# Loading the weights of a GRU kernel one contraction part at a time

## The chip, the core and the metric

The kernel runs on one core of a Trainium2 chip. The metric is device time in microseconds (us) of one execution. The core has TensorE (PE) for products, VectorE (DVE), ScalarE (ACT), GpSimd (POOL) and SyncE (SP). SP, ACT and POOL also issue DMA transfers, which sixteen DMA engines carry out.

## The reference

`x` has 16 sequences of 256 steps with 512 channels. It first goes through a causal depthwise convolution with 16 taps, taken from `cond`, and is added to itself. Then a GRU runs over the 256 steps, starting from `cond`, and its states are added again.

```python
x = x + conv(x, cond[:, None, :])            # 16 taps, per channel, causal
# per step, h from the step before, D = 512:
gi = x_t @ W_ih + b_ih                       # W_ih, W_hh: 512 x 1536, gates r, z, n
gh = h @ W_hh + b_hh
r = sigmoid(i_r + h_r); z = sigmoid(i_z + h_z)
n = tanh(i_n + r * h_n)
h = (1 - z) * n + z * h
x = x + h over all steps
```

All of it is float32. The weights are 6 MB, `x` is 8 MB.

## The kernel before

Channels are on partitions. A channel's number is j * 128 + q * 32 + l; it sits on partition 32 j + l in part q. So a product over all 512 channels is four products, kc = 0 to 3, one for each part q, and a weight tile such as `whh[g]` is [128 partitions, 4 parts, 512 columns], with row j * 128 + q * 32 + l of the matrix on partition 32 j + l, part q. There are five weight tiles: `wih_n` and `wih_rz` (the latter 1024 columns wide, two gates) for the input, and `whh[R]`, `whh[N]`, `whh[Z]` for the state.

`x` comes in 16 chunks of 16 steps. `load_x(c)` brings one chunk in eight transfers of 64 KB. `turn_units` transposes a chunk on VectorE, and `tap_units` adds the convolution's taps there (L265), one instruction for each tap and part. Chunk 0 has half of its convolution on TensorE (`conv_on_tensor`, L292). Three buffers hold loaded chunks.

The order on each engine is written out by hand (`manual_schedule`). The kernel has a head and then 256 steps. In the head, `mark` and `idle_products(PAD)` give TensorE small products at the very start (L356). Then come the convolution of chunk 0, the biases, the input products of n for the first eight steps (`ni_units`, L320, with `wih_n`) and those of r and z for the first pair of steps (`pair_units`, L383, with `wih_rz`). `bulk.run(0, HEAD)` then puts taps of chunk 1, up to a planned cost of `HEAD` us, on VectorE ahead of step 0; `Plan` hands the rest to the steps by their deadlines.

A `step` makes the state's products in the order r, n, z (`recurrent`, L418, 16 products for each gate, kc outside and j inside), then a share of the input products of later steps. ScalarE makes r (L435), VectorE r times the n products (`rn`, L444), its transpose, the sum `n`, ScalarE the tanh (L455) and z (L461), and VectorE the new state by a scan (L470). The next step's products wait for that.

The DMA issues stand in the queues in program order. SP has part of `cond`, of chunk 0 and chunk 1, the biases, the first two quarters of `wih_n` and of `wih_rz`, then one quarter of each `whh`, then chunk 4 (issued when chunk 1 is transposed), then chunks 2 and 3 (which wait for z of step 1), and later all other chunks and the stores. POOL has part of chunks 0 and 1, the other two quarters of every weight tile, and two memsets of `zero_z` between them. ACT has one quarter of each `whh`. The framework numbers the transfers over eight lanes for SP and ACT together and eight for POOL; a transfer waits for the one before it in its lane to land.

A quarter here is a j: 32 partitions, on each of them four pieces (q) of 512 or 1024 columns.

Of the kernel before, what the change touches and what calls it, by code (L numbers as in the profile page):

```python
# [30 lines left out]
P = 128  # L31
L = 32
GT = 8
R, Z, N = 0, 1, 2
CHUNKS = (16,) * 16
PAD = 108
HEAD = 9.3
SYNC = mybir.DependencyInfo(mybir.DependencyClass.Sync, mybir.DependencyReason.DATA)
Q_PE = (2, 3)
NI = 8  # L40
# [35 lines left out]
def conv_gru_kernel(  # L76
# [10 lines left out]
    nc = tc.nc  # L87
    B, T, C = x.shape
    K = cond.shape[0]
    NQ = C // P  # L90
# [4 lines left out]
    GP = GT // 2  # L95
    NG = T // GT
    NCH = len(CHUNKS)
# [21 lines left out]
    def load_x(c, queues=((nc.sync,), (nc.sync,)), behind=None):  # L119

        n = CHUNKS[c]
        t = xin.tile([P, max(CHUNKS) // 2, P], F32, tag="x_nat", name=f"x_nat_{c}")
        for s in range(2):
            for j in range(NQ):
                made = queues[s][j % len(queues[s])].dma_start(
                    out=t[32 * j + B * s : 32 * j + B * s + B, 0 : n // 2],
                    in_=x[:, starts[c] + s : starts[c] + n : 2, j * P : (j + 1) * P],
                )
                if s == j == 0 and behind is not None:
                    tc.add_manual_dep(made.ins, behind.ins.name, SYNC, reason="later in time")  # L130
        x_nat[c] = t
# [8 lines left out]
    for j in range(NQ):  # L140
        (nc.sync, nc.scalar)[j % 2].dma_start(
            out=cond_nat[32 * j : 32 * j + B, :], in_=cond[:, j * P : (j + 1) * P]
# [17 lines left out]
        out=b_two[1:2, 0 : 2 * C], in_=b_ih[0 : 2 * C].rearrange("(o c) -> o c", o=1)  # L160
    )
    nc.gpsimd.dma_start(
        out=bn_nat[0:P:L, :], in_=b_ih[2 * C : 3 * C].rearrange("(j c) -> j c", j=NQ)
# [3 lines left out]
    wih_rz = const.tile([P, NQ, 2 * C], F32)  # L167
    wih_n = const.tile([P, NQ, C], F32)
    whh = [const.tile([P, NQ, C], F32, name=f"whh_{g}") for g in range(3)]

    def load_weights(w_sb, w, g, queues):
        for j in (0, 2, 1, 3):
            queues[j].dma_start(
                out=w_sb[L * j : L * j + L],
                in_=w[j * P : (j + 1) * P, g * C : g * C + w_sb.shape[2]].rearrange(
                    "(q l) c -> l q c", l=L
                ),
            )


    for tile_of, g in ((wih_n, N), (wih_rz, R)):
        load_weights(tile_of, w_ih, g, (nc.sync, nc.sync, nc.gpsimd, nc.gpsimd))
    zero_z = [const.tile([P, NQ * B * 2], F32, name=f"zero_z_{i}") for i in range(2)]
    for t in zero_z:
        nc.gpsimd.memset(t, 0.0)
# [26 lines left out]
    def turn_units(c):  # L212

        def halo():
            xT[c] = xtp.tile([P, NQ, HALO + CMAX], F32, tag="xT", name=f"xT_{c}")
            if c:
                m = CHUNKS[c - 1] * B
                nc.scalar.copy(xT[c][:, :, 0:HALO], xT[c - 1][:, :, m : m + HALO])

        def turn(a):  # L220
            o = HALO + a * PAIR
            nc.vector.transpose(
                xT[c][:, :, o : o + GT * B].rearrange("p q (a r) -> p a q r", r=L),
                x_nat[c][:, a : a + GP].rearrange("p a (q l) -> p a q l", q=NQ),
            )
            if 2 * (a + GP) == CHUNKS[c] and 3 < c + 3 < NCH:
                load_x(c + 3)

        return [(0.0, halo)] + [
            (0.7, lambda a=a: turn(a)) for a in range(0, CHUNKS[c] // 2, GP)  # L230
        ]
# [46 lines left out]
    def conv_on_tensor():  # L278

        n = CHUNKS[0] * B  # L280
        diag = const.tile([P, len(Q_PE), K, P], F32)

        def weight(k, q):
            return condT[:, q, k : k + 1] if k < K - 1 else last1[:, q : q + 1]

        for i, q in enumerate(Q_PE):
            for k in reversed(range(K)):
                nc.scalar.activation(diag[:, i, k], ident, AF.Copy, scale=weight(k, q))
        for i, q in enumerate(Q_PE):
            acc = ps_ni.tile([P, CHUNKS[0] * B], F32, tag="pni", name=f"conv_{q}")  # L290
            for k in reversed(range(K)):
                nc.tensor.matmul(  # L292
                    acc[:, lag(k) : n],
                    lhsT=diag[:, i, k],
                    rhs=xT[0][:, q, HALO : k * B + n],
                    start=(k == K - 1),
                    stop=(k == 0),
                    skip_group_check=True,
                )
            evictions.append(lambda q=q, acc=acc: nc.scalar.copy(x1T[0][:, q, 0:n], acc[:, 0:n]))  # L300
# [46 lines left out]
    def mark():  # L347

        for i in range(2):
            nc.tensor.matmul(rz[i], lhsT=blank[:, 0:P], rhs=blank, start=True, stop=True)  # L350
            nc.tensor.matmul(nh[i], lhsT=blank[:, 0:P], rhs=blank[:, 0:P], start=True, stop=True)

    def idle_products(n):

        for _ in range(n):
            nc.tensor.matmul(  # L356
                spare[0:L, 0, 0:1], lhsT=blank[:, 0:L], rhs=blank[:, 0:1], start=True, stop=True
            )
# [17 lines left out]
    def pair_units(p):  # L376

        c, o = chunk_of(2 * p)

        def prod(kc):  # L380
            w_rz = wih_rz[:, kc].rearrange("p (g c) -> p g c", g=2)
            for j in range(NQ):
                nc.tensor.matmul(  # L383
                    rz[p % 2][32 * j : 32 * j + 32],
                    lhsT=x1T[c][:, kc, o : o + PAIR],
                    rhs=w_rz[:, :, j * P : (j + 1) * P],
                    start=False,
                    stop=False,
                    skip_group_check=True,
                )  # L390

        return [lambda kc=kc: prod(kc) for kc in range(NQ)]
# [143 lines left out]
    mark()  # L536
    idle_products(PAD)
    nc.tensor.drain()
# [14 lines left out]
                last1[:, q : q + 1],  # L553
            )
    conv_on_tensor()
    for g in (R, N, Z):

        load_weights(whh[g], w_hh, g, (nc.sync, nc.scalar, nc.gpsimd, nc.gpsimd))

    taps = [fn for i, (_, fn) in reversed(list(enumerate(tap_units(0)))) if i % NQ not in Q_PE]  # L560
    needed = (NI - 1) * (NQ - len(Q_PE))
# [23 lines left out]
    for c in range(1, NCH):  # L585
# [9 lines left out]
        if c == 1:  # L595
            for cost, fn in ahead:
                bulk.add(cost, due + GT // 2, fn)
    bulk.run(0, HEAD)

# [3 lines left out]
    for t in range(T):  # L603
        p, s = divmod(t, 2)
        if s == 0 and p + 1 < T // 2:
            of_pair = pair_units(p + 1)
        if t % NI == 0 and t + NI < T:
            of_block = ni_units(*blocks[t // NI + 1])

        def other_products():  # L610

            for units in (of_pair, of_block):
                for _ in range(2):
                    if units:
                        units.pop(0)()

        def bulk_work():

            quota = bulk.rate(t) + 2 * 0.7 / GT
            room = ROOM  # L620
            while late and (t >= T - 2 or room == ROOM):
                cost, fn = late.pop(0)
                fn()
                quota -= cost
                room -= cost
            bulk.run(t, quota, room)

        h = step(t, h, bulk_work, other_products)
        if t == 1:

            load_x(2, behind=of_z[0])
            load_x(3)
        if t == T - 3:
            late += out_units(NG - 1, 0, GP - 1)
        elif t % GT == GT - 1 and t < T - 1:
            late += out_units(t // GT)
        elif t == T - 2:
            late += out_units(NG - 1, GP - 1, GP, (0,))
# [30 lines left out]
```

## Time and profile before

| | |
|---|---|
| Median of three runs | 1045.49 us (1044.62 to 1045.6) |
| The profiled execution | 1043.0 us, its span 1041.2 us |
| Granted TensorE clock, mean | 0.999 |
| Busy | PE 98%, DVE 89%, ACT 37%, POOL 1% |
| HBM | 14.73 MB read, 8.39 MB written |

Times are from the start of the span. "Busy" is the time in which an engine has an instruction in execution. In the group rows the last column is the time for which the engine stood idle ahead of them, and what ended it. A DMA's time to landing runs from its issue to its completion. Here are the weights' issues:

| tile | issued by | number, size | median us to landing |
|---|---|---|---|
| wih_n | SP / POOL | 2 / 2, 256 KB | 8.8 / 7.7 |
| wih_rz | SP / POOL | 2 / 2, 512 KB | 15.3 / 11.3 |
| whh | SP / ACT / POOL | 3 / 3 / 6, 256 KB | 18.1 / 12.7 / 16.9 |

### The profile page before, as it was taken

Reading aid. Unit: us, or ns where it says so; the run is one execution under the profiler, and the core shown is the slowest. Engines: PE = TensorE matmul, PEld = TensorE weight load, DVE = VectorE, ACT = ScalarE, POOL = GpSimd, SP = SyncE. Lnnn points to the kernel's source line nnn. Section 1 sums busy time; section 2 is a strip of 40 time slices with the busy share of each in tenths; the row PEclk is TensorE's granted clock in tenths of the full one; section 3 lists DMA queues with packets and bytes.
Section 4 is the critical chain, followed back from the end, with each engine's and each line's share of the span. In section 5 each row is a group of like instructions: output and inputs, shape, how many; then the busy total and the mean of one; then the engine's idle time right before and its main releaser. Section 6 shows DMA issues by size and latency. Waiting matters only on the chain.

```text
span 1041.2 us, 71851 instructions
## 1 busy us (share of the span) xinstructions
PE 1021.8 (98%) x32952; PEld 927.2 (89%) x32952; DVE 925.6 (89%) x3606; ACT 380.5 (37%) x1520; POOL 11.4 (1%) x27
## 2 busy tenths in 40 slices
PE   7899999999999999999999999999999999999997
PEld 6689999999999999999999999999999999999986
DVE  7799999999999999999999999999999999896555
ACT  6243433434333343433334333343333334333332
POOL 4000000000000000000000000000000000000000
PEclk9999999999999999999999999999999999999999
DMA  9510100100010010100100010010000000000000
GB/s 222 124 38 8 31 14 20 30 15 26 13 34 15 15 34 6 35 14 15 35 14 25 14 33 17 14 35 5 14 15 14 14 13 6 14 15 14 14 10 17
DMA packets 40978, 27.72 MB, mean 27 GB/s; under 512 B 6686, under 2 KB 38498, under 8 KB 40676
## 3 DMA queue, kind: packets, MB, share of 16 engines
q1 hardware_dynamic: 38612, 18.52, 8.0%
q8 instruction: 257, 4.21, 1.8%
q0 software_dynamic: 1216, 3.67, 1.4%
q10 hardware_dynamic: 848, 0.95, 0.4%
q14 instruction: 45, 0.37, 0.1%
HBM read 14.73 MB, written 8.39 MB: 22 GB/s over the span
## 4 chain that ended last, share of the span: by engine, by line
PE 94%; DMA 3%; DVE 1%; ACT 0%; issue 0%; ACTq 0%; SPq 0%
PE prz L418 42%; PE pnh L418 21%; PE prz L383 20%; PE pni L320 10%; DMA whh<-in_L_cond_W_hh_dram 2%; DMA wih_n<-in_L_cond_W_ih_dram 1%; DMA x_nat<-in_x_dram 0%; DVE rn L444 0%; DVE rnT L446 0%; DVE zp L457 0%; ACT zero_z L461 0%; DVE n L448 0%; DMA out_dram<-o 0%; DVE hist L470 0%; DVE glance L398 0%
## 5 line engine op out<-in xcount | busy, mean ns | idle before, releaser
L418 PE MATMUL prz<-whh,hist 128*32 128x128 f32 x16320 | 539.4, 273 | 2.2 <-DVE hist L470 1.0
L418 PEld LDWEIGHTS prz<-whh,hist 128*32 128x32 f32 x16320 | 449.7, 104 | 7.5 <-DVE hist L470 5.2
L265 DVE SCALAR_TENSOR_TENSOR x1T<-xT,condT,x1T 128x256 f32<-128x256 f32 (+2 forms) x930 | 377.4, 461 | 0.6 <-ACT x1T L239 0.6
L383 PE MATMUL prz<-wih_rz,x1T 128*32 128x256 f32 x4096 | 267.8, 379 | 2.6 <-DMA wih_rz<-in_L_cond_W_ih_dram 2.6
L418 PE MATMUL pnh<-whh,hist 128*32 128x128 f32 x8160 | 269.5, 273 | 0.0
L418 PEld LDWEIGHTS pnh<-whh,hist 128*32 128x32 f32 x8160 | 226.5, 104 | 0.0
L455 ACT ACTIVATE dn<-n 128x64 f32<-128x64 f32 x256 | 67.9, 265 | 327.2 <-DVE n L448 327.2
L383 PEld LDWEIGHTS prz<-wih_rz,x1T 128*32 128x32 f32 x4096 | 128.3, 110 | 46.6 <-issue 2.9
L320 PEld LDWEIGHTS pni<-x1T,wih_n 128*32 128x32 f32 x4096 | 122.3, 110 | 43.0 <-ACT x1T L300 0.6
L435 ACT ACTIVATE r<-prz 128x128 f32<-128x128 f32 x256 | 71.1, 278 | 238.4 <-PE prz L418 235.6
L320 PE MATMUL pni<-x1T,wih_n 128*32 128x128 f32 x4096 | 157.6, 273 | 0.0
L470 DVE TENSOR_TENSOR_SCAN hist<-zero_z,dn 128x32 f32<-128x32 f32 (+1 forms) x768 | 128.6, 216 | 0.0
L444 DVE TENSOR_TENSOR rn<-r,pnh 128x128 f32<-128x128 f32 x256 | 72.2, 282 | 39.1 <-PE pnh L418 37.9
L461 ACT ACTIVATE zero_z<-zp 128x32 f32<-128x32 f32 x512 | 90.9, 226 | 8.7 <-DVE zp L457 2.1
L446 DVE STREAM_TRANSPOSE rnT<-rn 128x128 f32<-128x128 f32 x256 | 79.8, 312 | 8.8
L457 DVE STREAM_TRANSPOSE zp<-prz 128x128 f32<-128x128 f32 x256 | 80.8, 316 | 2.0 <-PE prz L418 2.0
L332 ACT ACTIVATE ni<-pni,bnT 128x128 f32<-128x128 f32 x128 | 47.2, 368 | 74.7 <-PE pni L320 74.7
L463 DVE TENSOR_TENSOR dn<-hist,dn 128x64 f32<-128x64 f32 x255 | 58.3, 229 | 11.7
L448 DVE TENSOR_TENSOR n<-rnT,ni 128x64 f32<-128x64 f32 x256 | 57.6, 225 | 8.9
L398 DVE COPY glance<-r 1x1 f32<-1x1 f32 x256 | 34.0, 133 | 26.4 <-ACT r L435 26.4
L371 ACT COPY prz<-b_rows 128x256 f32<-128x256 f32 x128 | 48.5, 379 | 0.0
L398 DVE COPY glance<-zero_z 1x1 f32<-1x1 f32 x256 | 36.3, 142 | 7.9 <-ACT zero_z L461 0.2
(51 smaller groups left out, 208.7 us busy)
## 6 DMA issues: line engine op xcount, KB each, us to landing
out_dram<-o SPq DMA_DIRECT2D x248, 32.0 KB, 1.7
x_nat<-in_x_dram SPq DMA_DIRECT2D x118, 64.0 KB, 2.9
whh<-in_L_cond_W_hh_dram POOLq DMA_DIRECT2D x6, 256.0 KB, 16.9
wih_rz<-in_L_cond_W_ih_dram POOLq DMA_DIRECT2D x2, 512.0 KB, 11.3
wih_rz<-in_L_cond_W_ih_dram SPq DMA_DIRECT2D x2, 512.0 KB, 15.3
whh<-in_L_cond_W_hh_dram ACTq DMA_DIRECT2D x3, 256.0 KB, 12.7
whh<-in_L_cond_W_hh_dram SPq DMA_DIRECT2D x3, 256.0 KB, 18.1
x_nat<-in_x_dram POOLq DMA_DIRECT2D x8, 64.0 KB, 5.4
```

What stands on the lines that cost most here:

```text
L265: nc.vector.scalar_tensor_tensor(out=x1T[c][:, q, to], in0=xT[c][:, q, k * B + to.start : k * B + n], scalar=condT[:, q, k : k + 1], in1=x ...
L320: nc.tensor.matmul(hold[q][32 * j : 32 * j + 32, 0:n], lhsT=wih_n[:, kc, j * P + q * L : j * P + q * L + L], rhs=x1T[c][:, kc, o : o + n], ...
L383: nc.tensor.matmul(rz[p % 2][32 * j : 32 * j + 32], lhsT=x1T[c][:, kc, o : o + PAIR], rhs=w_rz[:, :, j * P : (j + 1) * P], start=False, st ...
L398: nc.vector.tensor_copy(glances[i][0:1], of_scalar[0:1, 0:1])
L418: product = nc.tensor.matmul(dst[32 * j : 32 * j + m], lhsT=h[0](kc), rhs=whh[g][:, kc, j * P : (j + 1) * P], start=False, stop=(kc == NQ ...
L435: of_r = nc.scalar.activation(r, pr, AF.Sigmoid)
L444: nc.vector.tensor_mul(rn, r, pnh)
L446: nc.vector.transpose(rnT, by_part(rn))
L455: nc.scalar.activation(dn_v[:, :, :, 1], n, AF.Tanh)
L457: nc.vector.transpose(zp, by_part(pz))
L461: nc.scalar.activation(z_v[:, qs, :, 1], zp[:, qs, half], AF.Sigmoid) for qs in halves
L470: nc.vector.tensor_tensor_scan(hist_g[:, lo + at : lo + end], z[:, to], dn[:, to], 0.0, op0=ALU.mult, op1=ALU.add,)
```

## The change

Each weight transfer now brings one part q of the rows to all 128 partitions, instead of one j (32 partitions) with all four parts. Parts 0 and 2 go on SP, 1 and 3 on POOL; ACT issues none. All five tiles are issued in one go, in the order in which they are used, ahead of the memsets of `zero_z` and of the convolution. The places of the data in SBUF, and the sizes of the transfers, stay. Chunk 4 is no longer requested when chunk 1 is transposed but behind chunks 2 and 3, at z of step 1. `HEAD` goes from 9.3 to 11.0, and `PAD`, the number of idle products, from 108 to 112.

```diff
-PAD = 108
-HEAD = 9.3
+PAD = 112
+HEAD = 11.0
...
-    def load_weights(w_sb, w, g, queues):
-        for j in (0, 2, 1, 3):
-            queues[j].dma_start(
-                out=w_sb[L * j : L * j + L],
-                in_=w[j * P : (j + 1) * P, g * C : g * C + w_sb.shape[2]].rearrange(
-                    "(q l) c -> l q c", l=L
-                ),
-            )
-
-
-    for tile_of, g in ((wih_n, N), (wih_rz, R)):
-        load_weights(tile_of, w_ih, g, (nc.sync, nc.sync, nc.gpsimd, nc.gpsimd))
+    def load_weights(w_sb, w, g):
+
+        for q in range(NQ):
+            (nc.sync, nc.gpsimd)[q % 2].dma_start(
+                out=w_sb[:, q],
+                in_=w[:, g * C : g * C + w_sb.shape[2]].rearrange(
+                    "(j q l) c -> q j l c", q=NQ, l=L
+                )[q],
+            )
+
+    load_weights(wih_n, w_ih, N)
+    load_weights(wih_rz, w_ih, R)
+    for g in (R, N, Z):
+        load_weights(whh[g], w_hh, g)
...
-            if 2 * (a + GP) == CHUNKS[c] and 3 < c + 3 < NCH:
+            if 2 * (a + GP) == CHUNKS[c] and 4 < c + 3 < NCH:
                 load_x(c + 3)
...
     conv_on_tensor()
-    for g in (R, N, Z):
-
-        load_weights(whh[g], w_hh, g, (nc.sync, nc.scalar, nc.gpsimd, nc.gpsimd))
...
             load_x(2, behind=of_z[0])
             load_x(3)
+            load_x(4)
```

## The prediction, made before the changed kernel ran

> **What bounds the kernel now.** I read the page's groups first, then the chain of waits of the first 42 us, then the DMA view of the same stretch, and last the queue rows.
>
> ```profile
> PE 1021.8 (98%) x32952; PEld 927.2 (89%) x32952; DVE 925.6 (89%) x3606; ACT 380.5 (37%) x1520; POOL 11.4 (1%) x27
> ...
> L418 PE MATMUL prz<-whh,hist 128*32 128x128 f32 x16320 | 539.4, 273 | 2.2 <-DVE hist L470 1.0
> ...
> L383 PE MATMUL prz<-wih_rz,x1T 128*32 128x256 f32 x4096 | 267.8, 379 | 2.6 <-DMA wih_rz<-in_L_cond_W_ih_dram 2.6
> ```
>
> TensorE is busy nearly all the time, and the idle column says that over 256 steps it hardly waits (2.2 us before L418, half of it near the end). From the first product on the new state (37.66 us) to the end there are 255 steps in 1003.5 us, 3.94 us each, all products. Nothing in the diff touches those. So the change is worth what it does to the moment at which the last weights of step 0 are there. The chain of waits shows that moment:
>
> ```profile
> 7.17 11.41 DMA wih_n<-in_L_cond_W_ih_dram
> 18.57 0.02 issue
> 18.59 16.77 DMA whh<-in_L_cond_W_hh_dram
> 35.36 0.14 issue
> 35.49 1.07 PE prz L418 x32
> ```
>
> The z products of step 0 (35.49) wait for the last quarter of the z weights, which SP issued at 18.59, late, because it had to wait for wih_n to land (the waits of SP's queue: L173 waited for wih_n twice, 5.3 us the longer time). What the transfers wait for is the DMA engines themselves. From 10 to 34 us:
>
> ```profile
> DMA  9999999999999999999999999999999999999999
> GB/s 198 229 188 201 201 236 273 290 273 300 239 266 317 294 297 352 317 307 259 345 273 280 239 314 307 283 307 314 318 318 304 300 297 307 289 262 157 118 163 172
> ...
> q0 software_dynamic: 921, 3.10, 48.2%
> q1 hardware_dynamic: 1669, 2.49, 44.6%
> q10 hardware_dynamic: 432, 0.79, 11.9%
> ```
>
> All sixteen engines are full from 10 to 34 us. The head is bound by transfers, and a full engine moves 300/16 = 19 GB/s in the better slices. So the question is: on how many engines does a transfer of the new shape run?
>
> **How many engines a transfer takes.** The page's queue row for SP counts packets, and I can take them apart.
>
> ```profile
> q1 hardware_dynamic: 38612, 18.52, 8.0%
> ```
>
> SP issues 118 loads of x at 128 pieces of 512 B (15104), its stores (31 groups x 8 x 64 pieces, then 384, 64 and 32: 16352), seven weight transfers of 128 pieces (896), two of cond (32) and two of b_two (2). That is 32386. The remaining 6226 are completions: 389 transfers with 16 or 32 outer rows at 16 each are 6224, and 2 are left, one for each one-row b_two. So a transfer posts one completion for each engine it runs on; 16 or 32 outer rows take sixteen engines, one row takes one.
>
> The old weight transfer has outer count 32 on both sides (l, then q). The new one has 128 partitions on the SBUF side, and on the DRAM side j, l, c, whose outer count is 4 and can't be merged with the 32 (768 KB against 6 KB steps). No row shows two sides that differ. The bounds are four engines, if the smaller side decides, and sixteen, if the SBUF side does. I take four: b_two is the only row with an outer count under 16, and it ran on as many engines as that count. Nor does a row show whether four would be the same ones from one SP transfer to the next. If they changed in turn, the load would be even again, which is rival one's arithmetic; if not, it piles up. I take the same four, as a fixed place for each outer index is the plainer arrangement, and leave the other to the chances.
>
> The Trainium skill ("DMA: Bandwidth & Descriptors", section on why a DMA increments its semaphore by 16) speaks against this change: the engine count is the largest number up to 16 that divides the slowest dimension of both patterns, and on the hardware queues they are the lowest-numbered ones. By it every new SP transfer would sit on the same four engines; its ceiling of about 27 GiB/s an engine would make the 46 us below some 34, an estimate from that page that nothing here shows.
>
> **The change part by part.**
>
> *Weights in four engines.* SP carries half of the weights: two parts of each of wih_n, wih_rz and three whh, 0.52 + 1.05 + 3 x 0.52 = 3.15 MB. POOL carries as much. If its transfers also take four engines but in turn, or sixteen, a quarter of that, 0.79 MB, falls on SP's four. So 3.93 MB must pass four engines before the last z part of SP. Rate: in the stretch 24.5 to 29.9 us sixteen engines moved 306 GB/s, so four move 76.5 under load; at best a 2 KB packet of the trace took 84 ns, which is 24.4 GB/s an engine or 98 for four. With twelve engines nearly idle I take a value between, 85. That gives 3.93 MB / 85 GB/s = 46.2 us (bounds 40.3 and 51.4). The first wih_n packets on SP flow at about 8.0 us (issued 6.79 to 8.50), so the last z part lands at 54.2 instead of 35.36: +18.9 us.
>
> *Parts by kc.* `recurrent` goes through kc = 0 to 3 and each new transfer is one kc. When the last part lands (kc 2; kc 3 is POOL's), half of the 32 z products are done: 1.07 / 2, -0.5 us. In the before state the last quarter of j held up all 32.
>
> *Clock.* Between the parts TensorE would sit idle for 3 to 4 us at a time. The trace has one such case: the conv products began after 4.37 us idle, and their first half (32 records) took 6.0 us, the second half with the same shapes 4.65.
>
> ```profile
> L292 PE MATMUL conv<-xT,diag x64: 262/281/763, 9.4 to 19.8; 128*128 128x256 f32 x4, 128*128 128x240 f32 x4, 128*128 128x224 f32 x4, 128*128 128x208 f32 x4
> ```
>
> The 763 ns (a 128x256 product, 379 at L383) is the slow start. The granted-clock column says 1.00 throughout, so only the durations show it. One such start after the last wait: +1.4 us (0 to 1.7). The waits before it cost nothing more, as the last landing covers them.
>
> *HEAD 11.0.* `bulk.run(0, HEAD)` puts 32 taps of chunk 1 ahead of step 0 instead of 28, four more at 0.41 to 0.46: 1.7 to 1.85 us on VectorE. They ended at 30.34, and now at about 32.2. The first rn waits for the n weights, at 33.73 before and by the sum not before 45: cost nothing. With all weights there by 32 us they would be the next bound (rival one). The taps taken out of the later steps free VectorE, which TensorE doesn't wait for.
>
> *Fifth x chunk.* Eight loads, 0.52 MB, leave SP's place behind the weights (22.84 to 35.68) and come after chunks 2 and 3 at step 1. On sixteen full engines six of them took 0.39 MB / 300 GB/s = 1.3 us of the weights' time. With four engines the gain is a few tenths of that (they follow the weights on the queue), so nothing. Chunks 2 and 3 took SP 10.4 us (41.2 to 51.6); with chunk 4 about 16, from about 61 to 77. Chunk 2's transposes come in step 5 or later, now a step earlier for the four taps, more than 8 us after its own loads; chunk 4 is needed tens of steps later. Stores, which queue behind on SP, start at step 8 (about 88 us). Nothing waits.
>
> *Queues and the rest.* ACT loses three issues (0.3 to 0.45 us each, its sequencer ran ahead), SP's z issues wait for wih_n to land, about 15 us, and their packets would queue behind wih_rz anyway. POOL's two memsets of zero_z go behind its last issue, at 16 us or somewhat later; first use is at 37. Four more idle products are 4 x 28 ns in a gap of 4.37 us. All nothing.
>
> Sum: 18.9 - 0.5 + 1.4 = +19.8 us. On the profiled execution (1043.0 us; span 1041.2) that is 1062.8. The runs' median is 1045.49, 2.5 above the profiled one, so 1065.3.
>
> **The rivals.**
>
> One, all sixteen engines take part (other side: faster). For it: the SBUF side has 128 partitions, and each DMA has the same 256 or 512 KB. Then 0.39 MB of x no longer stand in the way (-1.3 us), and if 128 partitions take 300 GB/s where 8 to 14 us showed 206, another 0.56 MB / 300 = -1.9. The last z part then lands at 32.2 to 34; VectorE, free at 32.2 instead of waiting for 33.73, allows -1.5, and the rest only as far as z is the later. I put -2.2: 1043.3 (1041.5 to 1045). It decides if the last whh lands before 35.36. Against it: b_two's completion counts. 0.15.
>
> Two, four engines only for SP, and the packets at their shortest (84 ns for 2 KB), with POOL's share out of the way by other engines: 3.15 MB / 98 = 32.1, landing at 40.1, +4.7 - 0.5 + 0.7 = +5, 1050. This is the low end of the slower case. Part of the 0.81 below.
>
> Three, POOL's transfers too stay on those four: 6.3 MB / 85 = 74 us, +47 us, 1092. Nothing in the trace speaks for it, software transfers share evenly now. 0.04 within the slower case.
>
> Four, the two effects cancel, because eight engines share the load or the clock is kept: 1044 to 1047. 0.04.
>
> **How the numbers follow.** Four engines, in its variants: 0.81; no change: 0.04; sixteen: 0.15. 0.2% of 1045, about 2 us, is what a measurement of this kernel can tell from no change. The likeliest case with its bounds of rate (40.3 to 51.4 us) and clock gives +12.5 to +25.3, 1058 to 1071; POOL's unknown share stretches it to 1050 below and, with some of POOL's engines shared twice, 1084 above. The faster case is left out of the range, with the extreme of rival three: 0.2.
>
> **What would show it.** Right: the SP queue's row reads 38612 + 3 x 128 pieces - 112 + 40 completions = 38924 (39044 with sixteen engines); the DMA row falls to 3 to 5 tenths after some 25 us; SP's last whh takes over 30 us from issue to landing; the chain ends its DMA stretch at 48 to 60 us; the first products after it are slow for some 3 us; from there steps of 3.94 us. Wrong: DMA at 9 tenths to the end of the head, and z of step 0 before 36 us; or SP's transfers on four engines but over 100 GB/s for them.

## The result, and the profile after

The changed kernel's median is 1076.87 us, the kernel before in the same series 1045.18 us: ratio 1.0296, 95% interval 1.0279 to 1.0313. The median is of four executions, 1073.49, 1076.59, 1077.14 and one of 1221.54 at a granted clock of 0.841, which the ratio leaves out. The profiled execution took 1076.59 us (span 1074.8), 33.6 us more than the profiled one of before.

First the page, its engine row and the groups that answer to those shown of before:

```profile
PE 1030.1 (96%) x32956; PEld 930.1 (87%) x32956; DVE 926.8 (86%) x3606; ACT 380.3 (35%) x1520; POOL 12.7 (1%) x27
...
q1 hardware_dynamic: 38924, 19.30, 8.0%
q0 software_dynamic: 3520, 3.69, 2.5%
...
L420 PE MATMUL prz<-whh,hist 128*32 128x128 f32 x16320 | 539.4, 273 | 2.2 <-DVE hist L472 1.0
...
L385 PE MATMUL prz<-wih_rz,x1T 128*32 128x256 f32 x4096 | 270.7, 382 | 15.2 <-DMA wih_rz<-in_L_cond_W_ih_dram 15.2
```

The products on the state (L420, two lines lower than before) still take 273 ns each, with 2.2 us of idle time ahead of them: the 255 steps did not change. The idle time is new in the head, where wih_rz alone held TensorE up for 15.2 us. SP's queue row reads 38924 packets. POOL's row reads 3520; before it was 1216.

The chain of waits of the first 80 us, from the first weight issue that it holds:

```profile
10.04 7.00 SPq L174
17.03 0.04 issue
17.08 20.84 SPq L174
37.92 0.04 issue
37.96 6.86 SPq L174
44.82 0.04 issue
44.86 3.39 SPq L174
48.25 0.04 issue
48.29 5.08 SPq L174
53.37 0.04 issue
53.42 14.21 DMA whh<-in_L_cond_W_hh_dram
67.63 0.04 issue
67.67 1.05 PE prz L420 x16
68.73 1.71 PE prz L385 x16
70.43 0.85 PE pni L322 x16
```

The columns are start, duration and what. The last z part landed at 67.63, not at 35.36. It was issued only at 53.42: SP's issue instructions for `whh` (L174) are themselves blocked, one of them for 20.84 us, while packets of the transfers before them are still under way. The first products with the new state began at 71.06 (37.66 before), which is +33.4 us, all of the 33.6.

The DMA view of the same 80 us (each column 2 us; upper row the busy share of the sixteen engines in tenths):

```profile
DMA  0799989998999899972222222222222220000135
GB/s 0 158 133 167 127 123 154 149 120 169 182 113 86 90 123 102 131 93 88 104 100 104 96 100 102 98 96 94 96 98 98 98 97 37 8 4 0 37 92 144
```

The same view of before:

```profile
DMA  0699999999999999931002435110000000514220
GB/s 0 159 157 193 187 207 224 286 271 323 304 264 311 310 302 261 147 48 35 8 8 74 140 87 141 51 57 0 8 4 8 0 8 27 140 37 112 43 57 1
```

There are two stages. Until about 34 us all engines are full, yet move 86 to 182 GB/s; the same columns of before, as full, have 187 to 323 between 6 and 32 us. Then the share falls to 2 tenths and the rate stands at 94 to 104 GB/s for some 28 us. That is the picture of four busy engines out of sixteen at about 24.5 GB/s each.

### The profile page after: what moved, and what is told of

It is laid out like the page before. It is cut to its first block, busy times and chain, and to the rows that moved or that the text cites. A ratio compares the mean times of both kernels' runs of the same rounds, so it can differ in the third digit from the quotient of the medians.

```text
span 1074.8 us, 71852 instructions
## 1 busy us (share of the span) xinstructions
PE 1030.1 (96%) x32956; PEld 930.1 (87%) x32956; DVE 926.8 (86%) x3606; ACT 380.3 (35%) x1520; POOL 12.7 (1%) x27
## 3 DMA queue, kind: packets, MB, share of 16 engines
q1 hardware_dynamic: 38924, 19.30, 8.0%
q0 software_dynamic: 3520, 3.69, 2.5%
## 4 chain that ended last, share of the span: by engine, by line
PE 92%; SPq 4%; DMA 2%; DVE 1%; ACT 0%; issue 0%; DVEq 0%
PE prz L420 41%; PE pnh L420 21%; PE prz L385 20%; PE pni L322 10%; SPq L174 4%; DMA whh<-in_L_cond_W_hh_dram 1%; DMA x_nat<-in_x_dram 1%; DVE rn L446 0%; DVE rnT L448 0%; DVE zp L459 0%; ACT zero_z L463 0%; DVE n L450 0%; SPq L125 0%; DVE hist L472 0%; DMA out_dram<-o 0%
## 5 line engine op out<-in xcount | busy, mean ns | idle before, releaser
L420 PE MATMUL prz<-whh,hist 128*32 128x128 f32 x16320 | 539.4, 273 | 2.2 <-DVE hist L472 1.0
L420 PEld LDWEIGHTS prz<-whh,hist 128*32 128x32 f32 x16320 | 449.8, 104 | 7.7 <-DVE hist L472 5.3
L385 PE MATMUL prz<-wih_rz,x1T 128*32 128x256 f32 x4096 | 270.7, 382 | 15.2 <-DMA wih_rz<-in_L_cond_W_ih_dram 15.2
L420 PE MATMUL pnh<-whh,hist 128*32 128x128 f32 x8160 | 269.6, 273 | 0.0
L420 PEld LDWEIGHTS pnh<-whh,hist 128*32 128x32 f32 x8160 | 226.4, 104 | 0.0
L385 PEld LDWEIGHTS prz<-wih_rz,x1T 128*32 128x32 f32 x4096 | 128.6, 111 | 61.0 <-DMA wih_rz<-in_L_cond_W_ih_dram 16.4
L322 PEld LDWEIGHTS pni<-x1T,wih_n 128*32 128x32 f32 x4096 | 124.0, 111 | 48.4 <-DMA wih_n<-in_L_cond_W_ih_dram 4.8
L322 PE MATMUL pni<-x1T,wih_n 128*32 128x128 f32 x4096 | 160.0, 276 | 4.5 <-DMA wih_n<-in_L_cond_W_ih_dram 4.5
L459 DVE STREAM_TRANSPOSE zp<-prz 128x128 f32<-128x128 f32 x256 | 80.9, 316 | 4.6 <-PE prz L420 4.4
```

The costliest lines, as they stand in the source:

```text
L322: nc.tensor.matmul(hold[q][32 * j : 32 * j + 32, 0:n], lhsT=wih_n[:, kc, j * P + q * L : j * P + q * L + L], rhs=x1T[c][:, kc, o : o + n], ...
L385: nc.tensor.matmul(rz[p % 2][32 * j : 32 * j + 32], lhsT=x1T[c][:, kc, o : o + PAIR], rhs=w_rz[:, :, j * P : (j + 1) * P], start=False, st ...
L420: product = nc.tensor.matmul(dst[32 * j : 32 * j + m], lhsT=h[0](kc), rhs=whh[g][:, kc, j * P : (j + 1) * P], start=False, stop=(kc == NQ ...
L459: nc.vector.transpose(zp, by_part(pz))
```

## The experiments

The edits are against the changed kernel unless said otherwise. Theory A is that the count of four on the DRAM side (j) puts each of SP's transfers on the same four engines, and that this queue sets the end. The rivals put the loss on POOL's transfers, on the other edits, or on the distance between the rows; each expectation states its own. Where one run is given, it is a single time beside the median of the kernel before on the same chip.

**Which part of the change costs the time?** `quarters_all_early` keeps everything but the shape: quarters j again, in the new order and place, chunk 4 late.

```diff
-        for q in range(NQ):
-            (nc.sync, nc.gpsimd)[q % 2].dma_start(
-                out=w_sb[:, q],
-                in_=w[:, ...].rearrange("(j q l) c -> q j l c", ...)[q],
+        for j in (0, 2, 1, 3):
+            (nc.sync, nc.sync, nc.gpsimd, nc.gpsimd)[j].dma_start(
+                out=w_sb[L * j : L * j + L],
+                in_=w[j * P : (j + 1) * P, ...].rearrange("(q l) c -> l q c", l=L),
```

> The changed kernel with only the shape undone: 32 partitions a transfer, two on SP and two on POOL for every tile, all issued at once; chunk 4 late, HEAD 11.0, PAD 112 stay. If the shape is the whole loss: sixteen engines full to the end of the weights, chunk 4's 0.39 MB out of the way (1.3 us), last z quarter at 32 to 35 us, VectorE's four extra taps to 32.2: total 1042 to 1045, 0 to 3 us below before. If the other edits cost too: above 1046.

It took 1043.90 us against 1045.22, ratio 0.9986 (0.9975 to 0.9996). So the shape is the whole loss, and the other edits are worth a little. The head was not faster than that because its last z quarter landed at 35.73, when only SP's queue was left, and because the clock had gone down. The windows of its trace show this (the last columns are granted clock, DMA share, GB/s):

```profile
28.00:32.00 4.00, 1.30 (x33) 0.81 (x32) 4.00 (x11) 0.55 (x2) 0.00 (x0) 0.99 1.05 249
32.00:36.00 4.00, 2.04 (x36) 1.46 (x40) 0.57 (x3) 0.00 (x0) 0.00 (x0) 0.50 0.34 67
```

**Does SP's queue have four engines?** `parts_all_on_sp` issues all four parts on SP.

```diff
-            (nc.sync, nc.gpsimd)[q % 2].dma_start(
+            nc.sync.dma_start(
```

> All twenty part-shaped transfers on SP, none on POOL. Four fixed engines: 6.29 MB at 98 GB/s (84 ns for 2 KB) = 64 us, last z part at 72 to 75 us, total 1079 to 1084, DMA at 2 to 3 tenths all the way. If the four engines changed from transfer to transfer, DMA at 9 tenths and the landing near 36 us, total about 1045. If the part shape is slow without POOL beside it (66 GB/s as the mean of the changed kernel): 103 us, total about 1110. SP row of the queues: 38924 + 10 x 128 + 2 x 0 + 40 = 40244 with four engines.

It took 1083.02 us (before: 1045.22), with the last z part at 72.9.

```profile
DMA  0599322222222222222222222222222222220000
GB/s 0 142 202 190 89 100 99 98 98 103 90 102 113 100 104 102 104 102 102 102 97 107 98 97 98 98 97 98 98 98 98 97 97 98 98 90 7 12 0 0
```

With nobody else on the engines the share is 2 tenths and the rate some 98 GB/s from 10 to 70 us. SP's queue row counts 40244 packets, the number that four completions for each of the twenty transfers give. More transfers on SP made no difference to the share. A queue that worked off one transfer at a time, on four engines that change, would show the same share. The trace's packets speak against it: the other three completions of a transfer follow its first by 0.35, 0.63 and 0.88 us, nearly the same in each of the last twelve transfers, and a mean of 4.0 to 4.2 packets is in flight in every 4 us from 8 to 72 us. Four engines that each work through their own row of packets look like that, so every transfer used the same four.

**What do POOL's transfers of the new shape cost?** `sp_parts_pool_rows` leaves SP's two parts as changed, and brings POOL's two in transfers of 32 partitions. `pool_parts_sp_rows` does the reverse.

```diff
+            for j in (2 * i, 2 * i + 1):
+                nc.gpsimd.dma_start(
+                    out=w_sb[L * j : L * j + L, 1::2],
+                    in_=w[j * P : (j + 1) * P, cols].rearrange("(q l) c -> l q c", l=L)[:, 1::2],
+                )
```

> SP keeps its part-shaped transfers (parts 0 and 2); POOL carries parts 1 and 3 as four transfers of 32 partitions each, outer count 32 on both sides. Theory A (SP's part-shaped transfers sit on four fixed engines, and POOL's part-shaped ones, crowding the same engines and partitions, halved their rate up to 36 us): the four engines carry 3.15 + 0.79 MB at 76 to 98 GB/s, last z part at 48 to 60 us, total 1056 to 1069. Theory B (a software queue beside them is enough to slow the four engines, whatever its shape): landing at about 67 us as in the changed kernel, total about 1075.

> The reverse: POOL keeps its part-shaped transfers (parts 1 and 3), SP carries parts 0 and 2 as transfers of 32 partitions. Theory A with POOL's transfers going round all sixteen engines four at a time: the load is even, the head nearly that of before, last weights at 34 to 42 us, total 1043 to 1050. Theory B' (POOL's part-shaped transfers are slow by themselves, about 100 GB/s as in the changed kernel at 10 to 36 us): 8 + 6.3 MB / 120 GB/s = 60 us, total about 1068.

The first took 1066.89 us, the last z part came at 58.0 (before: 1045.22 us). The second took 1061.79, and the last part landed at 51.2. The DMA view of the first, then of the second:

```profile
DMA  0699986999544675222222222222100003535152
GB/s 0 156 127 146 163 160 174 208 204 203 144 125 142 178 184 166 102 98 102 104 99 103 98 98 98 98 98 98 41 0 12 0 9 98 139 85 142 43 137 65
```

```profile
DMA  0699999999999999999999998000003515142500
GB/s 0 153 125 155 157 131 167 172 199 155 163 189 160 172 179 170 160 133 134 110 153 171 161 110 147 5 0 12 0 8 104 148 38 144 41 133 58 140 19 8
```

SP's parts alone suffice for the long stretch at 2 tenths. POOL's new shape adds 67.6 - 58.0 = 9.6 us to the landing in the changed kernel. The second run shows POOL's fault by itself: no stage at 2 tenths, but sixteen full engines that move 157 GB/s (10 to 50 us, mean) where the old shape moved 280 (10 to 30 us of before).

`parts_all_on_pool` has all four parts on POOL:

```diff
-            (nc.sync, nc.gpsimd)[q % 2].dma_start(
+            nc.gpsimd.dma_start(
```

> All twenty part-shaped transfers on POOL, none on SP. If the part shape on POOL is slow by itself (the two runs with POOL parts moved 120 to 155 GB/s with all sixteen engines full, against 280 to 300 for 32-partition transfers): 6.29 MB at 120 to 155 GB/s = 41 to 52 us, last part at 49 to 62 us, total 1058 to 1072. If it is slow only beside SP's traffic: 300 GB/s, landing at 30 to 34 us, total 1041 to 1045.

It took 1066.28 us (before: 1045.43), with the last z part at 57.4. All sixteen engines were full from 10 to 54 us, at a mean of 140 GB/s. So POOL's transfers do spread over the engines, unlike SP's, and are slow all the same. The queue also carries thousands of packets of 4 and 8 bytes there, but they hold only 1.3 of the sixteen engines in the mean. It is the packets of 4 KB that are slow: 348 ns (median), against 166 in `consecutive_rows` below.

**Do POOL's transfers meet SP's on the same engines?** `pool_skips_first_four` inserts three transfers of 2 KB with four outer rows on POOL, to shift the turn in which its transfers take the engines.

```diff
+            at = skips.get((g, q, 1 if w is w_ih else 0))
+            if at is not None:
+                nc.gpsimd.dma_start(out=junk[at][0:P:L, :], in_=b_ih[2 * C : 3 * C]...)
```

> The changed kernel with three 2 KB loads of four rows put into POOL's queue, ahead of the second wih_rz part, the first whh[N] part and the last whh[Z] part. If POOL's four-row and part-shaped transfers take four engines each, going round (the bias load first), then in the changed kernel the second wih_rz part and the second whh[N] part (0.79 MB) sat on SP's four engines, which fits the two stretches of shared traffic at 36 to 45 and 50 to 55 us; the small loads move all POOL parts off them. Expected: SP's four engines carry 3.15 MB alone, last z part at 42 us if they run at 98 GB/s throughout, at 50 to 58 us if the crowd of POOL parts on the other twelve still slows them till then; total 1050 to 1067. If POOL's transfers are spread in another way: as the changed kernel, 67 us and 1076.

It took 1067.72 us, the last z part at 57.8: 9.8 us earlier, for three small transfers more. The packets in flight show the meeting. In the changed kernel, from 36 to 44 us, SP's weights had a mean of 2.0 in flight and POOL's 2.1, at a share of 2 tenths: together the four engines of SP. Here SP's had 3.9 in flight from 36 to 48 us, and POOL's ran beside them on other engines. So POOL's transfers each take four engines, in turn, and their turn had brought some of them onto SP's four. The Trainium skill ("DMA: Bandwidth & Descriptors", section on why a DMA increments its semaphore by 16) has this rule for software queues: that many consecutive engines from a cursor that goes round. The runs agree that the engines change in turn; that they are consecutive, no run shows.

What is left of the loss shows in the same run: from 12 to 36 us SP's four engines, with four packets of SP's in flight and so nobody else's weights on them, moved only 45 GB/s in the mean. Packets of 2 KB took 179 ns or more there (medians over 4 us) and 85 to 87 from 40 us on, with few of the other engines busy; in `parts_all_on_sp`, with nothing beside them, they took 84 to 87 from the start. So the full engines beside them slow them down.

**Is it the distance of the groups in DRAM?** `pitch_33_rows` reads the four groups of 32 rows 33 rows apart (198 KB) instead of 128 (768 KB). The weights are then other rows of the matrix.

```diff
+                in_=w[q * 120 : q * 120 + 132, ...].rearrange("(j l) c -> j l c", j=4)[:, 0:L],
```

> The changed kernel, but the four groups of 32 rows lie 33 rows (198 KB) apart in DRAM in place of 128 rows (768 KB); other weights are read (another function), outer count 4, queues, sizes and destinations stay. If the four-engine transfers of several groups hinder each other because of the 768 KB distance of their reads: POOL's parts run at the 4 KB packet's 230 ns or less, POOL is done by 25 us, SP's four engines run at 76 to 98 GB/s, last z part at 48 to 58 us, total 1056 to 1067. If it is the destination (engines of different groups write the same 32 partitions in the same order) or the shape itself: as the changed kernel, 65 to 69 us, 1074 to 1078.

It took 1073.98 us, the last z part at 64.5, again with full engines and 104 to 197 GB/s until about 32 us. So a distance of 768 KB is not the cause.

**Is it the count of four?** `consecutive_rows` reads 128 rows in a row for each part. The destination, the sizes and the queues stay; only the count on the DRAM side goes from 4 (x 32) to 128. The rows then land in other places than the kernel's channels have.

```diff
-                in_=w[:, ...].rearrange("(j q l) c -> q j l c", q=NQ, l=L)[q],
+                in_=w[q * P : (q + 1) * P, g * C : g * C + w_sb.shape[2]],
```

> The changed kernel, but each part transfer reads 128 consecutive rows of the matrix in place of its four groups of 32; the weights are then in other places (the result is another function), the bytes, queues, sizes and destinations are the same. The DRAM side's outer count is 128. If the outer count of 4 is the whole cause: sixteen engines on both queues, 280 to 300 GB/s, last z part at 32 to 35 us, total 1040 to 1044. If the 128-partition destination is what is slow: landing beyond 45 us, total above 1055. SP's queue row 39044, POOL's 1216 as before.

It took 1039.41 us against 1045.26: ratio 0.994 (0.9925 to 0.9955). Its DMA view of 10 to 34 us (0.6 us a column):

```profile
DMA  9999999999999999999999999711000100000000
GB/s 297 379 365 399 413 410 399 416 396 423 410 410 396 379 399 393 359 393 382 389 382 396 369 379 410 270 61 38 7 0 0 27 0 0 0 0 27 0 0 0
```

All weights were in by some 27.5 us. SP's row is 39044 packets, the number for sixteen engines. And 128 partitions take about 390 GB/s, where the quarters of 32 partitions took 256 to 293 from 14 to 30 us in `quarters_all_early`. The chain of waits has changed hands:

```profile
16.25 15.91 DVE x1T L265 x48
33.93 1.08 PE prz L418 x32
```

VectorE's taps, 32 of them chosen by `HEAD`, now end at 32.15 and set the start of the steps at 33.93, 3.7 us earlier than before.

**Can the kernel have that rate with the rows where it needs them?** `channels_interleaved` numbers the channels 4 l + q within each 128, so that a part is 128 rows at a pitch of four. Every transposition then reads with a stride of four elements (that of the output, L520, writes with it), and so does one weight load.

```diff
-HEAD = 11.0
+HEAD = 7.8
...
-        return natural.rearrange("p (q l) -> p q l", q=NQ)
+        return natural.rearrange("p (l q) -> p q l", q=NQ)
...
-                    "(j q l) c -> q j l c", q=NQ, l=L
+                    "(p q) c -> q p c", q=NQ
...
-                    lhsT=wih_n[:, kc, j * P + q * L : j * P + q * L + L],
+                    lhsT=wih_n[:, kc, j * P + q : (j + 1) * P : NQ],
```

> The changed kernel with the 128 rows of a part taken four rows apart: part q holds rows q, q+4, q+8 ... of its 512, so that the DRAM side of each of the twelve transfers counts 128 single rows, as in consecutive_rows, and not four groups. The order of channels inside each 512 is changed with it in the places that use it (the views of turn and store, the products of the n part), so that the whole reference is computed. HEAD is 7.8 more taps of chunk 1 as a hand-set figure. Theory A (the count of four in the DRAM side picks four engines, and nothing else is lost): all sixteen engines at 370 to 410 GB/s, SP's queue row at 39044 packets, the last weights in by 27 to 29 us, and VectorE's taps end last, at about 29 us in place of 32.1 of consecutive_rows; the first products with the state at 31 to 33 us in place of 37.66; steps afterwards of 3.94 us as before; 1037 to 1040 us. Rival: rows that lie 6 KB apart are slower than rows that lie side by side, or views with a stride of four cost VectorE's transposes or TensorE's weight loads something in each of the 256 steps: then the steps are over 3.94 us each, and 0.02 us a step are 5 us: over 1042 us.

It took 1063.72 us against 1046.16: ratio 1.0169 (1.0145 to 1.0192). The transfers did what theory A said (352 to 415 GB/s from 10 to 24 us, 39044 packets), and the first state products of step 1 began at 32.4. The rival took all of it back in the steps. Its page, then the same row of `consecutive_rows`:

```profile
DVE 47%; PE 46%; ACT 4%; issue 2%; DMA 1%; DVEq 0%; POOL 0%; SPq 0%; POOLq 0%
...
L448 DVE STREAM_TRANSPOSE rnT<-rn 128x128 f32<-128x128 f32 x256 | 108.1, 422 | 8.8
```

```profile
L446 DVE STREAM_TRANSPOSE rnT<-rn 128x128 f32<-128x128 f32 x256 | 79.7, 311 | 8.7
```

The transposition of rn, which each state waits for, takes 422 ns instead of 311; those of x (L224) take 1154 ns in the steps from 40 to 900 us, where `consecutive_rows` shows 688. VectorE now carries 47% of the chain that ended last, and a step takes (1061.9 - 32.4) / 255 = 4.04 us instead of 3.94. That is 26 us over the run; 0.111 us of rnT in 255 steps are 28. TensorE's weight loads (L420) waited for the new state for 25.8 us between 40 and 900 us, where `consecutive_rows` shows 0.2. They did so in only 87 of those steps, so the longer transpositions of x and of the output may have a part in it; no run separates them. The transposition of z (L459), which reads TensorE's output memory with the same stride, took 308 ns, no more than before (316). The weight load with the stride (L322, 136 ns instead of 110) shows no idle time behind it.

**What are the other edits worth?** Against the kernel before: `x4_late` only moves chunk 4; `x4_late_head` has `HEAD` and `PAD` as well; `x4_late_warm` adds idle products in the waits of step 0, to keep the clock up.

```diff
-            if 2 * (a + GP) == CHUNKS[c] and 3 < c + 3 < NCH:
+            if 2 * (a + GP) == CHUNKS[c] and 4 < c + 3 < NCH:
...
             load_x(3)
+            load_x(4)
```

> The kernel before with chunk 4 alone moved behind chunks 2 and 3. 0.39 MB less among the weights at 300 GB/s: the last z quarter 1.3 us earlier, 34.0 us; total 0.5 to 1.5 us below before. If chunk 4's loads only filled gaps: no change within 0.5 us.

> The kernel before with chunk 4 late, HEAD 11.0 and PAD 112, weights as before on three queues: the best of what is known. VectorE's taps ahead of step 0 end at about 32.2 us, before the first rn (33.7 less what the weights gain, about 32.5): as x4_late within 0.3 us if the weights set the end, up to 0.5 us slower if the taps do. 1043 to 1045.

> x4_late_head with 50, 20, 35 and 20 idle products (28 ns each) in front of the first wih_rz products and the r, n and z products of step 0, where TensorE waited 2.2, 0.8, 1.5 and 0.8 us. In some profiles the clock was halved after these waits (z products of step 0 1.57 to 1.91 us in place of 1.07). If the waits cause it: 0.3 to 1 us below x4_late_head, 1041.4 to 1042.2, with less spread. If the idle products don't count for the clock, or delay the first products where weights come early: 1042.4 to 1043.

| kernel | median, us | before, us | ratio (95%) |
|---|---|---|---|
| x4_late | 1042.31 | 1045.43 | 0.9974 (0.9962 to 0.9985) |
| x4_late_head | 1042.41 | 1045.43 | 0.9972 (0.9960 to 0.9983) |
| x4_late_warm | 1044.88 | 1045.26 | 0.9993 (0.9982 to 1.0005) |

Chunk 4 out of the weights' way is worth 3 us, more than I expected; `HEAD` and `PAD` add nothing to it that can be measured. They beat both kernels. The idle products were a miss, and the run does not test their idea. TensorE stood idle for 3.28 us in the midst of the 50 before the first wih_rz products, and this wait is not put down to any transfer; the parts of wih_rz had landed by about 26.5:

```profile
25.75 0.78 PE spare L356 x31
26.53 3.28 issue
29.81 0.59 PE spare L356 x17
30.40 3.49 PE prz L383 x30
```

In `x4_late_head` the same products began at 26.27. The granted clock fell to 0.50 from 30 to 34 us, and 30 products of r and z took 3.49 us, 116 ns each (16 of them take 0.86 us, 54 ns each, at full clock). Most of the 3 us were lost again. Whether idle products that fill a wait keep the clock up, this run can't tell.

## Why the prediction was right, and where it was not

**Four engines.** Right, and by the count that was named: 38924 packets in SP's row, 40244 with all parts on SP, 39044 where the DRAM side counts 32 or 128. That they are the same four each time, which was a choice and not a reading, is shown by `parts_all_on_sp`: 98 GB/s with twenty transfers on the queue, and the steady lags between the completions.

**The rate: the term that was mis-sized.** The forecast was +19.8 us, measured are +33.6. The parts of the measured sum are +32.3 for the landing, -0.5 for the half of z and +1.75 for the clock, so the landing has nearly all of the miss. The sum put 3.93 MB through the four engines at 85 GB/s (76.5 to 98) and landed at 54.2. The landing came at 67.63: 3.93 MB in 59.6 us are 66 GB/s, below the lower bound.

The packets of the trace divide this into two stages. From 8 to 36 us SP's weights moved at 31 GB/s (0.87 MB). From 36 to 66 us they and 0.71 MB of POOL's moved at 97 GB/s, more than the 85. So what failed is the ground given for the rate, "With twelve engines nearly idle": until 36 us the twelve were full with POOL's parts, and beside them the four made less than half of the lower bound. The 76.5 was taken from a row in which sixteen engines carried transfers of the old shape, and the new shape does not allow that rate.

9.6 of the 13.4 us too many go when POOL's parts are brought as rows: the same 3.93 MB then pass in 50 us, 79 GB/s, inside the bounds. As many go when POOL's turn is shifted away from SP's four engines; 0.79 MB at 85 GB/s would be 9.3. So the amount in "a quarter of that, 0.79 MB, falls on SP's four" was about right. But with four engines in turn, how much falls on SP's four, and when, depends on where the turn stands, and that it was a quarter here is chance.

The measured time is above the 1071 of the likeliest case. The range held it because it was stretched to 1084 for "some of POOL's engines shared twice", and that is not what happened: here the width helped, not the working.

**The stage in between was not foreseen.** "The DMA row falls to 3 to 5 tenths after some 25 us" was wrong in both parts: it stayed full until about 34 us, at roughly half the rate of before, and then fell to 2 tenths. Why several transfers of the new shape together slow down full engines to means of 126 to 157 GB/s stays open. A distance of 768 KB between the rows is excluded (198 KB gave nearly the same), and so is the time of POOL's small packets; four groups on the DRAM side with 128 partitions is what the slow runs share. Whether it is that several engines write the same partitions, or the order of the pieces, no run separates.

**Half of the z products.** Right: 16 products at 67.67 instead of 32.

**The clock.** Predicted +1.4, measured about +1.75: the z, r/z and n products between the landing and the next state took 3.39 us, against 2.17 before, of which half of z (0.5) is gone. The windows of the changed kernel show what the durations say:

```profile
30.00:40.00 10.00, 1.59 (x52) 1.30 (x44) 2.50 (x7) 0.73 (x2) 0.00 (x0) 0.67 0.65 104
40.00:50.00 10.00, 3.18 (x28) 1.19 (x32) 0.00 (x0) 0.00 (x0) 0.00 (x0) 0.50 0.26 100
50.00:60.00 10.00, 3.14 (x48) 1.27 (x44) 0.14 (x1) 0.55 (x2) 0.00 (x0) 0.50 0.26 97
60.00:70.00 10.00, 5.16 (x80) 2.71 (x76) 1.78 (x10) 0.61 (x3) 0.00 (x0) 0.50 0.19 68
70.00:80.00 10.00, 10.00 (x317) 8.80 (x312) 8.64 (x34) 2.57 (x11) 0.00 (x0) 0.94 0.20 55
```

The granted clock (third column from the end) is 0.50 from 40 to 70 us, and the 16 products at L385 took 1.71 us where the same 16 took 0.86 before.

**HEAD, chunk 4, the queues.** The four taps were hidden, as said. Chunk 4 late cost nothing in the changed kernel, but "nothing" was too low where the transfers are fast: beside the old weights it is a gain of 3 us. SP's blocked issues had been costed at nothing, and they are: the packets, not the instructions, are what is late, for SP's and POOL's together kept 3.9 to 4.2 in flight in every 4 us from 36 to 64 us. But two of the signs failed by them and by the rate. "SP's last whh takes over 30 us from issue to landing" measured 14.21, since that issue came only at 53.42, and the DMA stretch ended at 67.6, not at 48 to 60.

**Rival one** was wrong of this kernel and right of its mechanism. With sixteen engines (`consecutive_rows`) 128 partitions do take a higher rate, the landing is early, VectorE's taps become the bound, and the gain is 3.5 us between the profiled executions (5.9 between the medians), where it said 2.2. **Rival two** got its condition in `pool_skips_first_four`, with POOL's share off SP's engines, and landed at 57.8 instead of 40.1, since SP's four moved only 45 GB/s from 12 to 36 us, beside twelve full ones. Rivals three and four did not happen.

## What to carry to other kernels

Before reshaping a transfer, read the outer count of both of its sides: the smaller decided here how many engines worked, and the completions in the packet count of SP's queue tell it. A busy share of the engines is not a rate: full engines moved between 86 and 415 GB/s here, so a bound must come from a row with the same shape. And a view that makes the transfer good must be paid for where the data are used: 26 us in the steps for 5 in the head.

## What the runs showed of the hardware

- SP's transfers with a DRAM count of four ran on the same four engines, 98 GB/s together; POOL's took four in turn. POOL's row rose from 1216 to 3520 packets.
- 128 partitions took about 390 GB/s, 32 partitions some 290, with all engines full in both. Several transfers of four groups to 128 partitions made 126, 140 and 157 of the same sixteen (means of three runs).
- An issue instruction on SP was blocked for up to 20.84 us while its engines were full.
- VectorE's transposition of 128x128 (rn, from SBUF, the memory on the core) took 311 ns, with a stride of four elements on its input 422. The Trainium skill ("SBUF — State Buffer", the note on lines of 16 bytes in "Door 1: The DMA port swizzle") says that each access that crosses to a new line pays a penalty, and it counts strides as free up to "4 fp32". Four elements of float32 are 16 bytes, one line: the run agrees with the penalty, and its stride of four is not free.
